# A four-layer graph network on one core: the order of its 11,118 steps, kept as packed data in place of a rule of due times

## The chip, the core and the metric

The kernel runs on one core of a Trainium2 chip. The core has five engines that each work through their own queue of instructions in order: TensorE (PE in the profile) multiplies matrices, VectorE (DVE), ScalarE (ACT) and GpSimd (POOL) do the elementwise work, and SyncE (SP) only issues transfers. 16 DMA engines carry the transfers. TensorE's results go to eight PSUM banks; everything else lives in SBUF, or in DRAM. The metric is the device time of one execution in microseconds (us), the median of several runs.

## What is computed

32 graphs, each with N = 512 nodes, D = 256 features and an adjacency matrix `adj` of 512x512, go through four layers. Every layer ends as `x = layernorm(x + layer(x))`. All numbers are float32.

```
L0  h = relu(((1 + eps) * x + adj @ x) @ W1 + b1);  h @ W2 + b2              # hidden width 512
L1  h = x @ W, 4 heads of 64;  e[i,j] = leaky_relu(e_dst[i] + e_src[j], 0.2)
    softmax over j where adj > 0.5;  attn @ h + bias
L2  q, k, v = x @ Wq.T, x @ Wk.T, x @ Wv.T, 8 heads of 32
    softmax(q.k / sqrt(32) + log(adj + 1e-6)) @ v;  @ Wo.T + bo
L3  s = ((x @ W) @ x.T) * adj;  softmax over the nodes that the mask keeps;  s @ x
```

The kernel adds the logarithm of layer 2 as a factor: `exp(score) * (adj + 1e-6)`. Softmax sums are divided out after the multiplication with v or x.

## The kernel before

**Steps and graphs.** `fast_path` does the work. It does not write instructions at once, but describes them as steps of a `Plan`. A step has a name, an engine, an estimated cost in us, the names of the steps it comes after, the buffers it takes, and a function that emits its instructions. There are 33 sets of steps: one that prepares the weights, and one for each graph, with the same names in each (`s0` to `s7` are the scores of layer 2, `i0` and `i1` the projection of layer 3, `w0` to `w3` its output). In all there are 11,118 steps, 2,077 of them on TensorE. The program keeps several graphs in work at a time: while one graph is in its last layer, others are in the first three, so that TensorE always has a matmul of some graph to do. The stock of buffers limits this: 13 large ones (B), 12 middle ones (C), 10 strips (D), eight PSUM banks (p), 6 graphs alive, 7 score blocks of layer 2 and some more.

**How a graph goes through the engines.** The parts that the prediction speaks of, with their lines:

- The adjacency is loaded twice by SP: as it stands, and turned (`Ar`, L821), in four loads that read 32 columns each in pieces of 128 bytes. A load of x stands at L833.
- Layer 1 builds a row of node values (`R`, L1045 and L1052: written to DRAM, read back to all partitions), ScalarE and VectorE make the weights `z` from it (L1104, L1115), TensorE multiplies.
- Layer 2: eight score steps of four matmuls with 32 rows each into four banks (L1293), ScalarE's exponential (L1306), VectorE's multiplication with the adjacency (L1315), and eight attend steps (L1351). The sums over the keys that the softmax divides by are not all made on TensorE. POOL issues transfers that add one block of 128x2048 numbers (1 MB) to another in SBUF (`collect`, L1326: `cd1`, `cd3`, `cd5`, `cd7`, then `cd2` and `cd6`), and at last one that adds one half of the partitions to the other (`fd0`, `fd1`, L1379). A single TensorE step, `d2` (L1398), takes what is left of both halves, and VectorE applies the result (L1456). Only the very last graph makes these sums wholly on TensorE (L1420).
- The biases of the layers are added to x by POOL's transfers too (`bias_steps`, L625).
- Each layernorm (L655 to L684) makes `rstd` on POOL, `shift` on VectorE, and applies both on ScalarE.
- Layer 3 needs x turned. `turned` writes x to DRAM (L710), reads it back in four loads (L723) into `xL`, and VectorE transposes 32x32 blocks of it (L742) into `xT`. TensorE follows with the projection (`iT`, steps `i0` and `i1`), the scores (`s`, L1539) and the output (`o_ps`); the result is normalised and stored by SP (L1596).

**Modes of TensorE.** A step may run as a whole matmul of 128 columns or as four of 32 columns. Steps marked "any" take the form that is on already; others need one form. `product` does it:

```python
        if plan.mode != "c32":
            nc.tensor.matmul(out, lhsT, rhs, start=start, stop=stop)      # L342
            return
        for q in range(4):
            part = slice(32 * q, 32 * q + 32)
            nc.tensor.matmul(out[part], lhsT[:, part], rhs, start=start, stop=stop)   # L346
```

**What sets the order.** The order of all steps is found while the program is built. `Plan.order` is a list scheduler: it keeps the time at which every engine and buffer comes free by the estimated costs, and takes, among the steps that can start within a short time of the earliest one, the step with the least due time. The due time is the graph's turn times a period of 83.965 us, less the longest chain of steps that still follows, plus shifts by step name. These shifts are written in the call of `plan.run`: one list for all graphs, one for the first graphs, one for the last, and one each for single graphs. `Plan.run` then emits the steps in that order, and every engine does its instructions strictly in that order. A transfer is three steps: its issue on SP or POOL, a step of a made-up engine (`q1` for SP's, `qa` for POOL's accumulates) that stands for its time in the queue, and its landing. The issue and the queue step are ordered each for itself; only the issue is an instruction.

The block after the steps (from L1613) checks whether the fast path's number ranges were kept. If they were not, a second path (`general_path`) would run; it does not run with these inputs.

Of the kernel before, what the change touches and what calls it, by code (L numbers as in the profile page):

```python
# [12 lines left out]
AF = mybir.ActivationFunctionType  # L13
# [3 lines left out]
P = 128  # L17
# [19 lines left out]

class Step:
# [4 lines left out]
    def __init__(self, eng, us, after, take, mode, emit):  # L43
        self.eng, self.us, self.after, self.take, self.emit = eng, us, after, take, emit
        self.mode = mode
        self.then, self.frees = [], []


class Plan:
# [51 lines left out]
    def link(self):  # L101

        self.left = [{} for _ in self.steps]
        for g in reversed(range(len(self.steps))):
            steps, left = self.steps[g], self.left[g]
            for name, s in steps.items():
                for a in s.after:
                    (self.steps[0][a[1:]] if a[0] == "^" else steps[a]).then.append((g, name))
            for k, (_, after) in enumerate(self.frees[g]):
                for a in after:  # L110
                    steps[a].frees.append(k)
        for g in reversed(range(len(self.steps))):
            steps, left = self.steps[g], self.left[g]
            for name in reversed(steps):
                s = steps[name]
                left[name] = s.us + max(
                    (self.left[h][n] + self.hop(s, self.steps[h][n]) for h, n in s.then if h - g < 2),
                    default=0.0,
                )
# [6 lines left out]
    def ready(self, g, name, ends):  # L126

        s, t = self.steps[g][name], 0.0
        for a in s.after:
            h, n = (0, a[1:]) if a[0] == "^" else (g, a)  # L130
            t = max(t, ends[h][n] + self.hop(self.steps[h][n], s))
        return t

    def order(self, period, ahead, window, stay, rush=(), moves=(), edges=(0, (), 0, (), ())):


        room = {b: [(0.0, i) for i in range(n)] for b, n in self.stock.items()}
        engine, mode, out, last = {}, "", [], 0.0
        held = [{} for _ in self.steps]
        ends = [{} for _ in self.steps]  # L140
        waits = [{n: len(s.after) for n, s in steps.items()} for steps in self.steps]
        fwaits = [[len(after) for _, after in frees] for frees in self.frees]
        ready, low, opened = {}, 0, 0
        todo = [len(steps) for steps in self.steps]
        moved = dict.fromkeys((n for steps in self.steps for n in steps), 0.0)
        turn = [max(g - 1, 0) for g in range(len(self.steps))]
        for i, early in enumerate(rush):
            turn[-1 - i] -= early
        for n, far in moves:
            moved[n] += far  # L150
        lead, tail = edges[0], len(self.steps) - edges[2]
        early, late = dict(edges[1]), dict(edges[3])
        own = {g % len(self.steps): dict(far) for g, far in edges[4]}

        def shift(g, name):
            some = early if g <= lead else late if g >= tail else {}
            return moved[name] + some.get(name, 0.0) + own.get(g, {}).get(name, 0.0)

        def near(low):
            fill, until, between, left, drain = ahead  # L160
            return fill if low < until else drain if low >= len(self.steps) - left else between

        def open_to(n):
            nonlocal opened
            while opened < min(n, len(self.steps)):
                for name in self.steps[opened]:
                    if not waits[opened][name]:
                        ready[opened, name] = self.ready(opened, name, ends)
                opened += 1

        open_to(window)
        while low < len(self.steps):
            found = []
            for (g, name), t in ready.items():
                s = self.steps[g][name]
                t = max(t, engine.get(s.eng, 0.0))
                into = self.EITHER.get(mode, "c32") if s.mode == "any" else s.mode
                change = self.CHANGE[into] if s.eng == "pe" and into != mode else 0.0
                for k, (kind, _, rest) in enumerate(s.take):
                    r, n = room[kind], sum(b[0] == kind for b in s.take[:k])  # L180
                    if len(r) <= rest + n:
                        break
                    t = max(t, r[n][0])
                else:
                    due = turn[g] * period - self.left[g][name] + shift(g, name) + stay * change
                    found.append((t, due, g, name, change))
            if not found:
                return math.inf, out
            first = min(found)[0] + near(low)
            _, t, g, name, change = min((due, t, *f) for t, due, *f in found if t <= first)  # L190
            s = self.steps[g][name]
            t += change
            if s.eng == "pe":
                mode = self.EITHER.get(mode, "c32") if s.mode == "any" else s.mode
            del ready[g, name]
            got = {}
            for kind, key, _ in s.take:
                got[key] = held[g][key] = (kind, room[kind].pop(0)[1])
            if s.eng:
                engine[s.eng] = t + s.us  # L200
            end = ends[g][name] = t + s.us
            last = max(last, end)
            out.append((g, name, mode, got))
            for h, n in s.then:
                waits[h][n] -= 1
                if not waits[h][n] and h < opened:
                    ready[h, n] = self.ready(h, n, ends)
            for k in s.frees:
                fwaits[g][k] -= 1
                if not fwaits[g][k]:  # L210
                    key, after = self.frees[g][k]
                    kind, i = held[g].pop(key)
                    free = max(ends[g][a] + self.HOP.get(self.steps[g][a].eng, 0.0) for a in after)
                    room[kind].append((free, i))
                    room[kind].sort()
            todo[g] -= 1
            while low < len(self.steps) and not todo[low]:
                low += 1
                open_to(low + window)
        return last, out  # L220

    def run(self, tries):

        self.link()
        best = min((self.order(*t)[0], t) for t in tries)
        assert best[0] < math.inf
        for g, name, self.mode, got in self.order(*best[1])[1]:
            self.slot[g].update((key, i) for key, (_, i) in got.items())
            self.steps[g][name].emit()
# [3 lines left out]
def fast_path(  # L233
# [24 lines left out]
    B, N, D = x.shape  # L258
    NC = N // P
# [9 lines left out]
    sb = ctx.enter_context(tc.tile_pool(name="sb", bufs=1))  # L269
# [16 lines left out]
    selfw = const.tile([P, P], F32, name="selfw")  # L286
# [21 lines left out]
    def blk(i):  # L308
# [3 lines left out]
    plan = Plan({  # L312
        "B": 13, "C": 12, "D": 10, "p": 8,

        "live": 6, "L0": 1, "L1": 2, "L2": 2, "L3": 1, "AT": 4, "zs": 7, "edge": 1, "tmp": 2,
    })
# [280 lines left out]
    def graph(g):  # L597
        plan.graph()
        slot = plan.slot[-1]
        last = g == B - 1  # L600
        near = g < 2 or g >= B - 3
        t = {"g": g}
# [13 lines left out]
        def little(shape, tag, bufs=2):  # L616
            return small.tile(shape, F32, tag=tag, name=f"{tag}_{g}", bufs=bufs)
# [27 lines left out]
        def norm_steps(n, groups=(range(NC),), into=None):  # L645

            t[f"ve{n}"] = t[f"rstd{n}"] = t[f"shift{n}"] = None
            for k, group in enumerate(groups):
# [8 lines left out]
                @step(f"dev{n}.{k}", "pool", 1.1, (f"va{n}.{k}",) + prev(f"dev{n}.", k))  # L657
                def _(k=k, part=part):
                    if k == 0:
                        t[f"rstd{n}"] = little([P, NC], f"rstd{n}")  # L660
                    nc.gpsimd.tensor_tensor(  # L661
                        t[f"rstd{n}"][:, part], t[f"ve{n}"][:, part], nhalf[:, part], ALU.pow
                    )

                @step(f"sh{n}.{k}", "dve", 0.09, (f"dev{n}.{k}",) + prev(f"sh{n}.", k))
                def _(k=k, part=part):
                    if k == 0:
                        t[f"shift{n}"] = little([P, NC], f"shift{n}")
                    nc.vector.scalar_tensor_tensor(  # L669
                        t[f"shift{n}"][:, part], t[f"mv{n}"][:, part, 0], -1.0, t[f"rstd{n}"][:, part],  # L670
                        op0=ALU.mult, op1=ALU.mult,
                    )
# [1424 lines left out]
```

## Time and profile before

| | |
|---|---|
| median of 3 runs | 2766.87 us (2763.53 to 2771.05) |
| profiled execution | 2767.12 us |
| its span, first to last instruction | 2765.3 us |
| mean granted clock of TensorE | 0.994 |
| DMA traffic | 418.76 MB, mean 151 GB/s |
| read from and written to HBM | 155.53 MB and 31.24 MB |

The profile is of one execution. Its times are in microseconds. Engine names are those above; PEld is TensorE's loading of weights, which lies beside its matmuls. A name such as "iT_ps <- xT" gives the tile that an instruction writes and the ones it reads, by the program's names; L742 is line 742 of the kernel. A list of waits gives, for a group of instructions, the engine and tile that ended the idle time ahead of them, and how long that idle time was. The chain of work that ended last follows the last instruction back to what released it, step by step; its lines give start, length, and what ran. A window's line gives the busy time of each engine within it, the granted clock of TensorE (1.00 is full speed), the share of time that the DMA engines were busy, and GB/s. The hardware queues of SP's transfers are called hardware_dynamic, the queue of POOL's software_dynamic.

### The profile page before, as it was taken

The page shows a single profiled execution, that of the slowest core. Times are in us where ns is not written, and L with a number is a line of the kernel's source. Part 1 is how long each engine was busy: PE and PEld are TensorE (multiplying, and loading weights), DVE is VectorE, ACT ScalarE, POOL GpSimd, SP SyncE. Part 2 cuts the span into 40 slices and gives each one's busy share as a digit, 9 for nine tenths or more (in the row PEclk, how much of TensorE's full clock was granted, in tenths as well). Part 3 has the DMA queues.
Part 4 walks back from the last instruction along what each step waited for, and adds up shares of the span by engine and source line. Part 5 has one row for each costly group of instructions (what it writes and reads, how often), then busy time and mean ns, then how long its engine had stood idle before and what let it go on. Part 6 is the DMA issues. An engine that isn't in the chain of part 4 may idle for free.

```text
span 2765.3 us, 68089 instructions
## 1 busy us (share of the span) xinstructions
PE 2716.7 (98%) x28680; PEld 1317.9 (48%) x28680; DVE 2158.8 (78%) x4257; ACT 1720.4 (62%) x3320; POOL 474.8 (17%) x526
## 2 busy tenths in 40 slices
PE   8999999999999999999999999999999999899998
PEld 6544444444445444445444445444444443444443
DVE  3887778877879877879877879877878877578975
ACT  3676665666666666666666666666665665556853
POOL 1111211121111121111121111121111111111110
PEclk9999999999999999999999999999999999999999
DMA  8487787778888879888878888888896988736760
GB/s 167 80 168 150 148 168 147 160 160 163 158 163 151 171 157 169 162 156 153 174 162 160 149 171 151 171 157 169 155 163 135 182 168 163 156 73 146 155 131 17
DMA packets 476735, 418.76 MB, mean 151 GB/s; under 512 B 377788, under 2 KB 431496, under 8 KB 444552
## 3 DMA queue, kind: packets, MB, share of 16 engines
q0 software_dynamic: 45568, 277.89, 53.1%
q1 hardware_dynamic: 429872, 136.18, 24.2%
q8 instruction: 227, 3.72, 0.5%
q14 instruction: 84, 0.69, 0.1%
q10 hardware_dynamic: 984, 0.28, 0.0%
HBM read 155.53 MB, written 31.24 MB: 68 GB/s over the span
## 4 chain that ended last, share of the span: by engine, by line
PE 86%; DVE 6%; DMA 3%; issue 2%; ACT 1%; POOL 0%; SPq 0%; DVEq 0%; POOLq 0%; ACTq 0%
PE s L1293 8%; PE o_ps L1351 7%; PE v_ps L346 7%; PE y_ps L342 7%; PE o_ps L346 6%; PE o_ps L1137 6%; PE hT_ps L346 6%; PE s L346 5%; PE h1T_ps L346 4%; PE o2p_ps L346 3%; PE iT_ps L342 3%; PE s L342 3%; PE h1T_ps L342 3%; PE kT_ps L342 2%; DVE z L1115 2%; PE qT_ps L346 2%
## 5 line engine op out<-in xcount | busy, mean ns | idle before, releaser
L1315 DVE SCALAR_TENSOR_TENSOR z<-AT,z 128x1024 f32<-128x1024 f32 x512 | 612.6, 1214 | 108.2 <-ACT z L1306 107.0
L1306 ACT ACTIVATE z<-s 128x512 f32<-128x512 f32 x1024 | 541.4, 608 | 109.2 <-PE s L1293 103.4
L1104 ACT ACTIVATE z<-R_bc,nT,S 128x512 f32<-128x512 f32 x512 | 373.4, 807 | 72.0 <-DMA z<-z 58.2
L684 ACT ACTIVATE x<-x,shift,rstd 128x256 f32<-128x256 f32 x508 | 273.9, 593 | 179.6 <-DVE shift L669 174.8
L1115 DVE SCALAR_TENSOR_TENSOR z<-z,T,edge 128x512 f32<-128x512 f32 x512 | 346.5, 742 | 5.8 <-ACT z L1104 5.8
L1326 POOL DMA_DIRECT2D z<-z x186 | 174.4, 942 | 868.4 <-PE o_ps L1351 445.3
L661 POOL TENSOR_TENSOR rstd<-ve,nhalf 128x4 f32<-128x4 f32 (+1 forms) x131 | 169.0, 1339 | 854.8 <-DVE ve L655 846.6
L1293 PE MATMUL s<-qT,kT 32*128 32x512 f32 x2048 | 278.4, 626 | 0.4 <-ACT kT L1264 0.4
L1351 PE MATMUL o_ps<-z,v 128*32 128x512 f32 x2048 | 254.9, 599 | 2.6 <-DVE z L1315 1.4
L1539 DVE TENSOR_TENSOR z<-s,AT 128x512 f32<-128x512 f32 x128 | 88.4, 690 | 214.9 <-PE s L342 110.1
L1137 PE MATMUL o_ps<-z,v 128*32 128x512 f32 x2048 | 233.8, 595 | 2.5 <-DVE z L1115 2.5
L1165 DVE TENSOR_TENSOR z<-z 128x1024 f32<-128x1024 f32 (+1 forms) x256 | 229.5, 949 | 0.7 <-PE o_ps L1137 0.7
L638 DVE BATCH_NORM_STATS2 st<-x 128x6 f32<-128x256 f32 x508 | 212.7, 419 | 10.6
L346 PE MATMUL o_ps<-x,z 128*32 128x257 f32 x3520 | 202.4, 380 | 0.0
L346 PE MATMUL hT_ps<-AT,x 128*32 128x256 f32 (+2 forms) x2640 | 185.5, 380 | 0.0
L342 PE MATMUL y_ps<-w_sb,h1T 128*128 128x256 f32 x832 | 184.4, 379 | 0.0
L342 PEld LDWEIGHTS y_ps<-w_sb,h1T 128*128 128x128 f32 x832 | 156.1, 190 | 21.5 <-issue 1.0
L1293 PEld LDWEIGHTS s<-qT,kT 32*128 32x128 f32 x2048 | 96.7, 184 | 143.5 <-issue 63.6
L346 PEld LDWEIGHTS o_ps<-x,z 128*32 128x32 f32 x3520 | 114.8, 110 | 83.8 <-issue 6.9
L346 PE MATMUL h1T_ps<-hT,w_sb 128*32 128x512 f32 x1296 | 147.9, 595 | 0.0
L625 POOL DMA_DIRECT2D x<-biases x96 | 103.8, 1081 | 237.0 <-issue 67.7
L346 PE MATMUL s<-iT,xT 128*32 128x512 f32 x1232 | 139.4, 592 | 0.1
(188 smaller groups left out, 3858.7 us busy)
## 6 DMA issues: line engine op xcount, KB each, us to landing
z<-z POOLq DMA_DIRECT2D x186, 1024.0 KB, 8.7
x<-biases POOLq DMA_DIRECT2D x96, 512.0 KB, 9.6
R_bc<-R_dram SPq DMA_DIRECT2D x32, 1024.0 KB
Ar<-in_adj_dram SPq DMA_DIRECT2D x124, 256.0 KB
z<-z POOLq DMA_DIRECT2D x62, 512.0 KB, 7.7
x<-in_x_dram SPq DMA_DIRECT2D x32, 512.0 KB
out_dram<-x SPq DMA_DIRECT2D x31, 512.0 KB
x_dram<-x SPq DMA_DIRECT2D x27, 512.0 KB
```

Of the source, the lines that this page charges most:

```text
L342: nc.tensor.matmul(out, lhsT, rhs, start=start, stop=stop)
L346: nc.tensor.matmul(out[part], lhsT[:, part], rhs, start=start, stop=stop)
L638: nc.vector.bn_stats(t[f"st{n}"][:, c, :], t["xo" if n == 4 else "x"][:, c, :D])
L684: nc.scalar.activation(t[into][:, c, :D] if into else xn, xn, AF.Identity, bias=t[f"shift{n}"][:, c : c + 1], scale=t[f"rstd{n}"][:, c : c ...
L1104: nc.scalar.activation(t[f"e{h}"][:, c, :], t["Rbc"][:, h, :], AF.Relu, bias=t["nT"][:, h, c : c + 1], scale=t["S"][:, h, c : c + 1],)
L1115: nc.vector.scalar_tensor_tensor(z, z, t["T"][:, h, c : c + 1], t["edge"][:, c, :], op0=ALU.add, op1=ALU.mult)
L1137: nc.tensor.matmul(po[32 * q : 32 * q + 32, :], t["v"][:, c, hp * P + 32 * q : hp * P + 32 * q + 32], t[f"e{2*hp+q//2}"][:, c, :], start=( ...
L1165: nc.vector.tensor_add(z[:, :m, :], z[:, :m, :], z[:, m : 2 * m, :])
L1293: nc.tensor.matmul(pk, t["k"][hs, o, blk(c)], t["q"][hs, o, :], start=True, stop=True)
L1306: nc.scalar.activation(t[f"E{k}"][:, j, :], t[f"ps{k}{j}"], AF.Exp, scale=QSCALE)
L1315: nc.vector.scalar_tensor_tensor(z, t["AT"][:, c, None, :].to_broadcast([P, 2, N]), ADJ_EPS, z, op0=ALU.add, op1=ALU.mult,)
L1351: nc.tensor.matmul(t[f"n{o}"][32 * j : 32 * j + 32, :], t["v2"][:, c, o * P + F2 * j : o * P + F2 * (j + 1)], t[f"E{k}"][:, j, :], start=( ...
```

## The change

The rule of due times, its tables and the list scheduler are removed. In their place a constant `ORDER` holds the whole sequence of 11,118 steps: base-85 text of compressed bytes. For each place in the sequence it has two bytes, one in the first half of the data and one in the second: how far the step's graph lies ahead of the lowest graph that still has steps left, and the step's place among those that this graph has left. `Plan.sequence` unpacks it, and `Plan.run` follows it. `run` still keeps estimated times, but only to choose which of the free buffers a step gets; and it still sets TensorE's mode from the steps as they come. By its description the sequence was searched in four stretches. A second edit gives the small tiles `rstd` and `shift` of the last layernorm three buffers in place of two.

The steps themselves, their costs and what they come after are unchanged. Read step by step, the sequence has the same 2,077 TensorE steps as before. They stand in another order from the start to TensorE step 1,199, and from step 1,677 to the end; the 478 between them (of graphs 18 to 26, counted from 0) stand as they did. The lines of the kernel after are 31 higher than those before, from `fast_path` on.

```diff
+ORDER = (
+    'c-rk;>6+U}a?Cn$k>J%WX*8=h@%um5W<+Fx==Ip%?;HQJMX9?<0tBkEG9x38VoE6)e*D2FU!IOv>B}q2{ty58$XUlT9(spo`WraM'
...
+)
...
-    def ready(self, g, name, ends):
...
-    def order(self, period, ahead, window, stay, rush=(), moves=(), edges=(0, (), 0, (), ())):
...
+    def sequence(self, text):
+        data = zlib.decompress(base64.b85decode(text))
+        left, low = [list(steps) for steps in self.steps], 0
+        for ahead, place in zip(data[: len(data) // 2], data[len(data) // 2 :]):
+            g = low + ahead
+            yield g, left[g].pop(place)
+            while low < len(left) and not left[low]:
+                low += 1
+        assert low == len(left)
+
+    def run(self, text):
+
+        self.link()
         room = {b: [(0.0, i) for i in range(n)] for b, n in self.stock.items()}
...
+        for g, name in self.sequence(text):
             s = self.steps[g][name]
-            t += change
-            if s.eng == "pe":
-                mode = self.EITHER.get(mode, "c32") if s.mode == "any" else s.mode
...
+            t = engine.get(s.eng, 0.0)
+            for a in s.after:
+                h, n = (0, a[1:]) if a[0] == "^" else (g, a)
+                t = max(t, ends[h][n] + self.hop(self.steps[h][n], s))
             for kind, key, _ in s.take:
-                got[key] = held[g][key] = (kind, room[kind].pop(0)[1])
+                free, i = room[kind].pop(0)
+                t = max(t, free)
+                held[g][key] = kind, i
+                self.slot[g][key] = i
+            into = self.EITHER.get(self.mode, "c32") if s.mode == "any" else s.mode
+            if s.eng == "pe" and into != self.mode:
+                t += self.CHANGE[into]
+                self.mode = into
+            end = ends[g][name] = t + s.us
             if s.eng:
...
+                engine[s.eng] = end
+            s.emit()
...
-        best = min((self.order(*t)[0], t) for t in tries)
-        assert best[0] < math.inf
-        for g, name, self.mode, got in self.order(*best[1])[1]:
-            self.slot[g].update((key, i) for key, (_, i) in got.items())
-            self.steps[g][name].emit()
...
-                        t[f"rstd{n}"] = little([P, NC], f"rstd{n}")
+                        t[f"rstd{n}"] = little([P, NC], f"rstd{n}", 2 + (n == 4))
...
-                        t[f"shift{n}"] = little([P, NC], f"shift{n}")
+                        t[f"shift{n}"] = little([P, NC], f"shift{n}", 2 + (n == 4))
...
-        plan.run([(83.965, (0.0968633, 4, 1000000000.0, 9, 0.0348847), 6, 4.208, ...
+        plan.run(ORDER)
```

## The prediction

> **What bounds the kernel now.** I read the page first, then the chain of work that ended last, then TensorE's waits, then windows, and last SP's and POOL's own instructions.
>
> ```profile
> span 2765.3 us, 68089 instructions
> ...
> PE 2716.7 (98%) x28680; PEld 1317.9 (48%) x28680; DVE 2158.8 (78%) x4257; ACT 1720.4 (62%) x3320; POOL 474.8 (17%) x526
> ```
>
> TensorE is the bound: it is idle for 2765.3 - 2716.7 = 48.6 us in all. The chain shows the beat:
>
> ```profile
> 497.40 7.15 PE v_ps L346 x128
> 580.36 7.15 PE v_ps L346 x128
> 663.33 7.15 PE v_ps L346 x128
> ```
>
> The same piece comes back every 82.97 us, and so up to about 2118 us: one graph per 82.97 us. The window of one beat has no idle TensorE and a full clock, two windows of the last stretch do not (columns: stretch, length, busy time of PE, PEld, DVE, ACT, POOL, PE's clock, DMA share, GB/s):
>
> ```profile
> 497.00:580.00 83.00, 83.00 (x922) 40.14 (x918) 67.77 (x133) 53.40 (x104) 14.23 (x16) 1.00 0.81 156
> 2280.00:2300.00 20.00, 16.55 (x205) 7.37 (x196) 17.75 (x31) 8.82 (x16) 3.56 (x3) 0.91 0.98 154
> 2380.00:2400.00 20.00, 13.04 (x40) 5.12 (x41) 3.76 (x7) 4.02 (x10) 1.68 (x2) 0.83 0.77 153
> ```
>
> So the beat has nothing to give but mode changes, and what a new order can win lies in the filling (to 480 us) and the emptying (from 2124 us). I priced every TensorE step by its start-to-start interval in the beat (score step 0.96, attend step 0.86, FFN, projection or aggregation steps 1.72 to 3.46, output step 1.74, transposes 0.44, a mode change 0.09 to 0.11). The 2077 steps of the old order come to 2685.3 us. What the trace took beyond that:
> - from the first matmul (4.5 us) to 42.3 us: 11.0 (first loads, half clock until 17.7 us). It stays: the same loads come first.
> - 42.3 to 480.3: 15.9.
> - the beat to 2124: 1.8, nearly all at 2121 to 2124, in steps whose order is not changed. It stays.
> - 2124 to the last output step at 2750.7: 34.0, of which the last two waits (0.9) stay, being a chain without other work.
>
> **What the change removes.** The order of both built programs shows that the change does what it says: the same 2077 TensorE steps, in another order up to step 1199 (graph 18, counted from 0) and from step 1677 (graph 26) on; between them nothing moves. Mode changes fall from 541 to 512: 29 at 0.105 us are 3.0 us. No matmul columns, no transfer and no DVE or ACT work is added or taken away; ORDER is read while the program is built. The third buffer for the last layer's rstd and shift adds no instruction. Were every wait of the filling and emptying gone and no other came, the span would be 2765.3 - 3.0 - 15.9 - 33.1 = 2713.3 us. That is the floor. One of the waits is far the longest:
>
> ```profile
> PE iT_ps L346 <- DVE xT L742: 8.0, 1, 8.0
> ```
>
> **What the change adds: transfers come together.** The new order is tight for TensorE, so DMA decides.
>
> ```profile
> q0 software_dynamic: 45568, 277.89, 53.1%
> q1 hardware_dynamic: 429872, 136.18, 24.2%
> ```
>
> POOL's queue moves 277.89 MB in 0.531 x 2765.3 = 1468 us of all 16 engines: 5.5 us for a 1 MB accumulate (collect), 2.8 us for a half one (bias, or fd, the last half of a layer-2 sum). In the trace's landings its 344 transfers all come in the order of issue. The old rule and the new data both let a transfer's queue step stand elsewhere than its issue, so a gap-free plan is no proof. And the beat itself is tight: the last accumulate (L1379) lands 0.4 to 3.7 us before d2, the matmul on it.
>
> (1) The sum before d2. Per graph three accumulates follow each other: cd7, cd6, fd1. In the beat, counted from score step s7: cd7 is issued at 14.1 us; 1.0 issue + 5.5 + 1.8 landing and reissue + 5.5 + 2.8 (a bias ahead) + 2.8 + 2.3 landing give 35.8, the trace has 38.3; so I add 2.5 for SP's traffic. d2 stands at 40.6. The new POOL order gives:
> - graph 0: cd7 cd2 cd6, a bias, fd0, a bias, fd1 = 3 x 5.5 + 4 x 2.8 = 27.7 from 9.0 on: 42.5 against 38.5, 4.0 late.
> - graph 2: cd2 cd7 cd6 and five halves, 30.5 from 12.1 on: 48.4 against 46.4, 2.0 late.
> - graph 28: cd5 and four halves stand ahead of cd7, a bias ahead of fd1: 43.0 against 36.4, 6.6 late.
> Sum 12.6. Bounds: none late (without the 2.5 it is 1.5 + 0 + 4.1 = 5.6) up to twice as much, 25.
>
> (2) The turned x of layer 3: x3 is written to DRAM (L710), read back in four loads (L723), transposed (L742), then iT. One graph of the beat first:
>
> ```profile
> 1363.01 0.57 SPq L710 DMA_DIRECT2D x_dram<-x  x1
> 1370.47 8.34 SPq L723 DMA_DIRECT2D xL<-x_dram  x4
> 1378.99 6.69 SPq L821 DMA_DIRECT2D Ar<-in_adj_dram  x4
> ```
>
> (SP's instructions in order of time: start, length, what.) And from the chain of waits, the place that cost 8 us:
>
> ```profile
> 2363.80 4.56 SPq L723
> 2368.40 5.02 DMA xL<-x_dram
> 2373.42 1.12 DVE edge L1088 x3
> 2374.54 11.47 issue
> ...
> 2386.10 0.72 DVE xT L742
> 2386.82 0.14 issue
> 2386.96 3.41 PE iT_ps L346 x16
> ```
>
> In the beat the four adjacency loads (Ar, 1 MB in 128-byte pieces) stand behind the read; DVE transposes at 1385.2, 7.0 us after the last load is issued at 1378.1. At 2386 four Ar loads and an x load stood right ahead of the write, and the last load, issued at 2368.4, took 17.6. The new SP order puts 3 or 4 Ar loads between write and read for graphs 2, 7, 14, 15, 16 and 26 (the old: never over one). Four cost between 6.7 (SP's own issue time above) and 17.6 - 7.0 = 10.6; I take 8.7, three 6.5. Off come 2.0 that the landing has to spare in the beat (0.0 to 3.4) and the room between the last projection and iT over the beat's 40.5: +9.3, -1.7, +2.6, +1.7, +4.6, -1.0. Late by 0, 8.4, 4.1, 5.0, 0 and 5.5 to 7.5 (a write behind loads too), say 6.5: sum 24. Bounds: 0 (the next graph in the old order, with such loads ahead, did not wait) and 6 x 9.7 = 58 (the shown wait with its slow clock).
>
> (3) The clock. Behind waits of 1.3 to 3.1 us at 212, 2294, 2513 and 2646 us the clock record shows half speed for 3.4 us (the 0.91 windows), 1.7 us of work lost each. Seven waits from (1) and (2): 12; bounds 0 and 9 x 3.4 / 2 = 15. The Trainium skill, "TensorE: Matmul & The Clock Gate", Part 1, has the clock fall after an idle window of about 3.4 us. By that page only the six waits over 3.4 us would pay, an estimate of 10.2 in place of 12; the trace has it behind 1.3 us, so the trace decides.
>
> (4) Small late starts, 0.1 to 1 us, where a bank or an eviction comes a little late: the old order lost about 16 us by these in its 700 unrepeated steps, 0.023 each, and none in the beat. 1550 steps are unrepeated now: between 0 and 35. I take 17, halfway, since the old unrepeated steps and the beat are equally near.
>
> Sum: 2713.3 + 12.6 + 24 + 12 + 17 = 2778.9 us of span. The profiled execution took 2767.12 for a span of 2765.3, so 1.8 lies around it: **2780.7 us**. The median of the runs, 2766.87, is 0.25 below that execution; I leave that out. In the filling and emptying nothing hides these waits: TensorE has no other step in its order, and its queue is strict, so whatever stands behind d2 or iT waits too. DVE has the same: xT behind an unlanded load holds up the scores' multiplications.
>
> The skill's "DMA: Bandwidth & Descriptors", Queues, rings and completion order, says that completion is not FIFO per issuing engine. On POOL's queue this trace never shows it; on SP's only rows of 1 KB overtake. By that sentence a late half could pass others and (1) would shrink to nothing, an estimate of 2768 with the rest as it is.
>
> **Rivals.**
> - *The order holds* (faster). The transfers fit, because room was added elsewhere (graph 2 has 9.3 us more). Then 2713.3 + one wait such as the shown 9.7 + half of (4) 8.5 + 1.8 = 2733. For it: TensorE's order has no hole, and the emptying now has 8 to 10 us more between the last projection and iT than at the place that waited (29.8 there). Against it: the queues above. It decides once the waits of (1) to (4) sum to less than 2758.6 - 1.8 - 2713.3 = 43 us. Chance 0.27.
> - *Gain and loss cancel*: (1) and (2) at half and the clock at five falls: 2713.3 + 6.3 + 12 + 8.5 + 17 + 1.8 = 2758.9, and from there to 2775. Chance 0.13.
> - *Loads run into each other* (much slower): each of the six places costs 10.6 + 1.7, (1) doubles, (4) is 35: 2713.3 + 74 + 25 + 5 + 35 + 1.8 = 2854; half way there is 2817. Against it: a stalled TensorE issues fewer transfers. Chance over 2815: 0.08.
>
> **Numbers.** 0.3% of 2766.87 is 8.3 us, about what a measurement can tell from no change. Forecast, 2775 to 2815: 0.52; above: 0.08; so slower 0.60, same 0.13, faster 0.27. The range leaves out the top 0.08 and the best part of the order holding (under 2733, about 0.12): 2733 to 2815. Its slower part alone is 2775 to 2815.
>
> **What would show it.** TensorE's waits should name the accumulates into z ahead of the two-bank d_ps (L1398) (graphs 0, 2, 28) and DVE xT ahead of iT_ps several times, with a 0.83 or 0.91 clock behind each; between graphs 19 and 25 the beat must still be 82.97 us. If the waits of TensorE sum to under 30 us, and none is over 3 us, I am wrong and the order holds. If waits are many but short, (4) was the size, not the queues.

## The result, and the profile after

| | before | after |
|---|---|---|
| median | 2766.09 us (4 runs, 2763.53 to 2771.05) | 2812.91 us (4 runs, 2810.28 to 2818.31) |
| profiled execution | 2767.12 us | 2818.31 us |
| span | 2765.3 us | 2816.5 us |
| mean granted clock | 0.994 | 0.986 |

The kernel became slower by 46.8 us: the ratio is 1.017, with a 95% interval of 1.0149 to 1.019. The forecast was 2780.7, some 14 us above the kernel before, so the sign was right and the size less than a third of what it is. From the page of the profile after:

```profile
span 2816.5 us, 68977 instructions
...
PE 2726.0 (97%) x29112; PEld 1328.7 (47%) x29112; DVE 2152.0 (76%) x4257; ACT 1714.0 (61%) x3320; POOL 481.0 (17%) x526
```

TensorE is now idle for 2816.5 - 2726.0 = 90.5 us in place of 48.6. Its list of waits says for whom (total, times, longest):

```profile
PE d_ps L1429 <- DMA z<-z: 15.7, 2, 10.1
PE iT_ps L373 <- DVE xT L773: 15.7, 3, 8.2
PE iT_ps L377 <- DVE xT L773: 13.3, 2, 8.3
...
PE y_ps L373 <- DVE y L1241: 4.5, 1, 4.5
PE hT_ps L377 <- DMA x<-in_x_dram: 4.2, 1, 4.2
PE d_ps L1429 <- issue: 3.7, 1, 3.7
```

The first two groups are those that the prediction named: d_ps behind the accumulates into z, three times (graphs 0, 2 and 28), and iT_ps behind xT, five times (graphs 2, 9, 15, 25 and 26; the prediction had not named 9 and 25). The third new thing is a load of x that comes late (graph 17). The beat is untouched, and the stretches behind the waits run at a lower clock (windows: stretch, length, busy time of the engines, clock, DMA share, GB/s):

```profile
1740.00:1823.00 83.00, 83.00 (x922) 40.34 (x918) 67.88 (x134) 53.53 (x105) 14.87 (x16) 1.00 0.88 161
2350.00:2370.00 20.00, 14.77 (x34) 6.93 (x35) 10.94 (x31) 4.34 (x9) 1.93 (x2) 0.74 0.49 89
2580.00:2600.00 20.00, 10.67 (x164) 4.93 (x168) 6.24 (x18) 7.43 (x12) 1.88 (x2) 0.74 0.43 96
```

Two places show how a transfer comes late. First SP around the layer-3 input of graph 7 (start, length, what):

```profile
787.90 0.58 SPq L741 DMA_DIRECT2D x_dram<-x  x1
792.12 16.71 SPq L852 DMA_DIRECT2D Ar<-in_adj_dram  x3
808.99 2.62 SPq L754 DMA_DIRECT2D xL<-x_dram  x3
811.66 0.86 SPq L852 DMA_DIRECT2D Ar<-in_adj_dram  x1
812.56 1.83 SPq L754 DMA_DIRECT2D xL<-x_dram  x1
```

The write had landed by 793.6, but three Ar loads stood ahead of the read, and SP spent 16.71 us on issuing them; the third alone held it for 11.98 us. The prediction had 6.7 to 10.6 us for four. Then POOL around the sums of graph 28 (in brackets: idle time before, and what ended it):

```profile
2544.26 0.86 POOL L1357 DMA_DIRECT2D z<-z  x1 [5.75 <-PE o_ps L1382]
2544.79 1.22 POOL L656 DMA_DIRECT2D x<-biases  x1
...
2546.53 2.15 POOL L656 DMA_DIRECT2D x<-biases  x1
2550.47 0.82 POOL L1410 DMA_DIRECT2D z<-z  x1 [1.79 <-DMA z<-z]
2551.01 1.21 POOL L656 DMA_DIRECT2D x<-biases  x1
2551.58 1.54 POOL L1357 DMA_DIRECT2D z<-z  x1
2571.36 0.86 POOL L1357 DMA_DIRECT2D z<-z  x1 [18.25 <-DMA z<-z]
...
2583.20 0.82 POOL L1410 DMA_DIRECT2D z<-z  x1 [9.90 <-DMA z<-z]
```

These are cd5, four halves (three biases and fd0), cd7, cd6 and fd1. cd6 waits for cd7, which is 19.5 us on its way: cd5 and the four halves, issued just ahead of it, landed one after another from 2555.3 to 2565.9, and cd7 at 2571.1. Then cd6 itself takes 11.6 us, while SP's 1 MB load R_bc, issued at 2571.13, is under way too.

**The ledger** sets each TensorE step's time up to the next step against its price. By the prices of the prediction the new steps come to 2682.2 us, as forecast. Against the floor of 2713.3 the span is 103.2 us longer: 19.4 in waits ahead of d_ps (1); 29.0 + 4.5 + 4.2 = 37.7 in waits for xT, behind xT on VectorE, and for the late x (2); 19.9 of extra time in the steps right behind these waits, at half speed (3); the remaining 26.2 is (4), with some 6 of it inside the three d2 steps. The forecast had 12.6, 24, 12 and 17, which makes 65.6. (The profiled execution is 5.4 us above the median.)

### The profile page after: what moved, and what is told of

The parts are those of the page before. It is cut to its first block, busy times and chain, and to the rows that moved or that the text cites. A ratio compares the mean times of both kernels' runs of the same rounds, so it can differ in the third digit from the quotient of the medians.

```text
span 2816.5 us, 68977 instructions
## 1 busy us (share of the span) xinstructions
PE 2726.0 (97%) x29112; PEld 1328.7 (47%) x29112; DVE 2152.0 (76%) x4257; ACT 1714.0 (61%) x3320; POOL 481.0 (17%) x526
## 3 DMA queue, kind: packets, MB, share of 16 engines
q1 hardware_dynamic: 429872, 136.18, 24.3%
## 4 chain that ended last, share of the span: by engine, by line
PE 47%; DMA 3%; DVE 2%; issue 1%; ACT 1%; SPq 1%; POOL 0%; POOLq 0%; DVEq 0%; ACTq 0%
PE s L1324 5%; PE o_ps L1382 4%; PE o_ps L1168 4%; PE v_ps L377 3%; PE hT_ps L377 3%; PE o_ps L377 3%; PE h1T_ps L377 3%; PE y_ps L373 2%; PE s L377 2%; PE s L373 2%; PE o2p_ps L377 2%; DMA z<-z 2%; PE iT_ps L373 2%; PE y_ps L377 1%; PE kT_ps L373 1%
## 5 line engine op out<-in xcount | busy, mean ns | idle before, releaser
L1337 ACT ACTIVATE z<-s 128x512 f32<-128x512 f32 x1024 | 547.6, 607 | 164.2 <-PE s L1324 158.4
L692 POOL TENSOR_TENSOR rstd<-ve,nhalf 128x4 f32<-128x4 f32 (+1 forms) x131 | 177.8, 1372 | 857.8 <-DVE ve L686 786.0
L1196 DVE TENSOR_TENSOR z<-z 128x512 f32<-128x512 f32 (+1 forms) x256 | 232.3, 951 | 14.3 <-PE o_ps L1168 12.9
L377 PE MATMUL hT_ps<-AT,x 128*32 128x256 f32 (+2 forms) x2736 | 193.1, 383 | 0.0
L377 PEld LDWEIGHTS o_ps<-x,z 128*32 128x32 f32 x3584 | 117.4, 110 | 90.7 <-issue 14.3
L969 ACT ACTIVATE h1T<-h1T_ps,b_sb 128x512 f32<-128x512 f32 x128 | 87.0, 688 | 120.3 <-PE h1T_ps L377 70.6
L373 PE MATMUL y_ps<-w_sb,h1T 128*128 128x256 f32 x656 | 148.4, 385 | 4.5 <-DVE y L1241 4.5
L1168 PEld LDWEIGHTS o_ps<-z,v 128*32 128x32 f32 x2048 | 69.9, 110 | 141.4 <-issue 114.2
L373 PEld LDWEIGHTS y_ps<-w_sb,h1T 128*128 128x128 f32 x656 | 124.8, 193 | 21.7 <-DVE y L1241 5.2
```

The source lines that it names most:

```text
L1168: nc.tensor.matmul(po[32 * q : 32 * q + 32, :], t["v"][:, c, hp * P + 32 * q : hp * P + 32 * q + 32], t[f"e{2*hp+q//2}"][:, c, :], start=( ...
L1196: nc.vector.tensor_add(z[:, :m, :], z[:, :m, :], z[:, m : 2 * m, :])
L1337: nc.scalar.activation(t[f"E{k}"][:, j, :], t[f"ps{k}{j}"], AF.Exp, scale=QSCALE)
```

## The experiments

Ratios are to the kernel before, timed on the same chip. The kernel after (2812.91) was timed apart from the experiments; the median of the kernel before was between 2764.25 and 2766.09 us in every timing. "In the ledger" always means the one profiled execution.

### The four stretches alone

Both orders have done the same steps at four points, so they can be exchanged between them. The expectations name wrong TensorE steps for these points: they lie at steps 335, 751, 1218 and 1675, not at 160, 355, 1199 and 1677. By the same ledger, cut where the points really are, the stretches take 447.9, 540.8, 598.3 and 559.9 us before and 460.3, 553.3, 624.3 and 561.2 after: +12.4, +12.5, +26.1 and +1.3.

```diff
-stretches: new new new (same) new
+s1_only:   new old old (same) old
+s2_only:   old new old (same) old
+s3_only:   old old new (same) old
+s4_only:   old old old (same) new
```

> The kernel after with the new order in its first stretch alone (TensorE steps 0 to 160, about the first 215 us), the old order in all others. Both orders have done the same steps at the borders of the stretches, so they can be exchanged there. Theory A (each stretch brings its own losses, as the ledgers of the two profiles have them: 218.2 us to the border after, 215.1 before): +3 us, 2769. Theory B (the losses come from transfers that one stretch leaves in the queues for the next): under +1 us here, the loss shows only with the new order behind it.

> The new order in the second stretch alone (TensorE steps 160 to 355, about 215 to 480 us). Theory A: 270.8 us in place of 263.4, so +7.4 us, 2773.5, with the waits ahead of d_ps of graph 2 and iT of graph 2 as in the profile after. Theory B: well under that, +3 us or less.

> The new order in the third stretch alone (TensorE steps 355 to 1199, about 480 to 1574 us, where the old order ran its beat). Theory A: 1134.9 us in place of 1095.4, so +39.5 us, 2805, nearly all of the change's loss. Theory B: half of that or less.

> The new order in the last stretch alone (TensorE steps 1677 to 2077, from about 2198 us on). Theory A: 555.9 us in place of 554.7, so +1 us, 2767: what the new order wins by its closer packing (some 29 us of waits that are gone) it loses in three waits of 6 to 10 us (iT of graphs 25 and 26, d_ps of graph 28) with their slow clock. Theory B: the three waits are smaller here, and it is faster than before by 5 us or more.

| stretch | median | against before | ratio (95%) |
|---|---|---|---|
| s1_only | 2780.53 | +16.3 | 1.0058 (1.0041 to 1.0075) |
| s2_only | 2776.81 | +12.6 | 1.0049 (1.0032 to 1.0066) |
| s3_only | 2787.09 | +22.8 | 1.0089 (1.0072 to 1.0106) |
| s4_only | 2759.47 | -4.8 | 0.9987 (0.9977 to 0.9996) |

The four differences add up to 46.9 us, and the whole change costs 46.8. So in the main each stretch carries its own losses: theory A, once the borders are right. It is not exact: s1_only costs 3.9 us more than its ledger, s3_only 3.3 less, and the last stretch by itself is a small gain where the ledger has +1.3, which is nearer to what theory B said of it. There the wait ahead of iT of graph 25 is 2.5 us in the ledger, in place of 8.4 in the kernel after, with the same order but other times at which the transfers meet. Three quarters of the loss, 35.4 us, lie in the second and third stretch (452 to 1591 us), where the old order lost 1.0 us in all by the ledger, so that next to nothing could be won.

### Thin transfers

```diff
-                src, dst = (t[f"E{b}"].rearrange("p h n -> p (h n)") for b in (k, a))
+                src, dst = (t[f"E{b}"].rearrange("p h n -> p (h n)")[:, :N] for b in (k, a))
...
-                    nc.gpsimd.dma_start(z[dst], z[src], accum_op=ALU.add)
+                    nc.gpsimd.dma_start(z[dst, :N], z[src, :N], accum_op=ALU.add)
...
-                        t["Ar"][q].rearrange("j c (b i) -> j c b i", i=32),
...
+                        t["Ar"][q],
+                        adj[g][P * a : P * a + P].rearrange("(c j) n -> j c n", j=32),
```

The first two edits are those of a_pool, a_both and b_pool: they leave out three quarters of the sums of layer 2. The third is that of a_ar and a_both: rows of the adjacency stand where turned ones belong. b_pool has the old order.

> The kernel after with every accumulate of layer 2 (L1357 and L1410: cd and fd) cut to its first quarter: the same instructions and waits, a quarter of the bytes. It leaves out three quarters of the terms that the softmax of layer 2 divides by. Theory 1 (POOL's transfers and SP's share the DMA engines, and the new order lets them meet): the waits ahead of d_ps (28 us of loss with their slow clock) go, and most of the waits ahead of iT, y_ps and hT too (some 58 us), since SP's loads and stores drain faster: 2735 to 2755. Theory 2 (SP's loads hold themselves up, by their order and their small pieces): only the 28 us go, 2785. Theory 3 (engines stand in a wrong order, whatever the transfers cost): within 8 us of 2813.

> The kernel after with the four adjacency loads Ar (L852) in pieces of 2 KB in place of 128 bytes: the same bytes, tiles and instructions, but rows of the adjacency where turned ones belong, so layers work with another adjacency. Theory 1 (the loads' bytes meet POOL's bytes): little, 2800 or more. Theory 2 (the small pieces hold SP's queue up, between the write and the read of x): the waits of graphs 2, 7, 15 and 26 behind Ar loads go, 34 us with their clock, those ahead of d_ps stay: 2779.

> Both edits at once in the kernel after: accumulates of a quarter, Ar loads in pieces of 2 KB. Theories 1 and 2: no wait of TensorE on a transfer is left after 60 us, and the order is near its floor: 2725 to 2740 (2713 is the floor, 1.8 lie around it, and the small late starts, 10 to 20, stay). Theory 3: within 8 us of 2813.

> The old order with the accumulates cut to a quarter (and the third buffer of rstd and shift). If the old order loses to engines and not to transfers, as its list of waits says, little is won: its one wait on a transfer after 60 us (8 us and 1.5 of clock) may go, so 2754 to 2767. If cheap accumulates help whatever the order (theory 3's reading of a gain in the first run), it is faster by as much as the kernel after is.

| kernel | median | against before | ratio (95%) |
|---|---|---|---|
| a_pool | 2727.08 | -38.8 | 0.9860 (0.9840 to 0.9879) |
| a_ar | 2787.38 | +21.5 | 1.0086 (1.0065 to 1.0108) |
| a_both | 2727.82 | -38.0 | 0.9861 (0.9842 to 0.9880) |
| b_pool | 2748.87 | -17.0 | 0.9938 (0.9918 to 0.9957) |

With a quarter of POOL's bytes the new order gains 85.8 us on itself, the old one 17. TensorE's list of waits of a_pool begins with these lines (line numbers shift a little from kernel to kernel with the length of ORDER):

```profile
PE AT_t L880 <- DMA A<-in_adj_dram: 6.8, 3, 3.6
PE hT_ps L369 <- DMA x<-in_x_dram: 5.2, 1, 5.2
PE ok_ps L1645 <- DVE okr L1643: 3.4, 1, 3.4
PE y_t L1231 <- ACT z L1333: 1.1, 2, 0.8
```

The first two lie in the first 17 us, the third at the very end. d_ps and iT are gone as waits on transfers, though not one of SP's loads was changed: on average the write of x3 landed 5.0 us after its issue in place of 8.0, and an Ar load 6.4 in place of 8.2. So theory 1 holds, with a time below its range of 2735 to 2755, and theory 3 falls: with thin accumulates the new order is 21.8 us faster than the old one. Its span, 2725.3, lies 12.0 above the floor.

a_ar falls between theories 1 and 2: 25.5 us faster than the kernel after, of the 34 that theory 2 gave. SP's mean time to issue an Ar load fell from 2.13 to 0.63 us, yet it landed 6.5 us after its issue. From the issue of the write to the landing of the last read, graphs 2, 7, 15 and 26 still took 27.5, 26.7, 27.2 and 29.2 us, the beat takes 20. The small pieces are a part of it; with the accumulates thin they are worth nothing (a_both as a_pool).

### One queue's order alone

```diff
 SP (h_sp), graph 7; graphs 2, 14, 15, 16 and 26 alike
 write of x3 (graph 7)
-Ar loads (graph 11)
 four reads of x3 (graph 7)
+Ar loads (graph 11)
...
 POOL (h_pool), graph 2; graphs 0 and 28 alike
 cd6, fd0
-bias, bias, bias
 fd1
+bias, bias, bias
```

> The kernel after, with SP's order alone changed: for graphs 2, 7, 14, 15, 16 and 26 the adjacency loads Ar that stood between the write of x3 (L741) and its four reads (L754) stand behind the reads. TensorE's, VectorE's, ScalarE's and POOL's orders stay. Step (2) of the prediction (those loads hold up the read): the waits of graphs 2, 7, 15 and 26 go, with their clock 7.9 + 7.5 + 9.8 + 9.0 = 34 us in the ledger, so about 2779. Rival (it is POOL's accumulates that delay write and read, the loads between matter little): under 12 us, 2800 or more.

> The kernel after, with POOL's order alone changed: the biases (x<-biases, half-size accumulates) that stood between cd7 and fd1 of graphs 0, 2 and 28, two, three and one of them, stand behind fd1. Step (1) of the prediction (halves ahead of fd1 delay d2 by about 2.8 us each): the loss at graphs 0 and 2 (7.3 and 8.3 us) nearly goes, that of graph 28 (12.8) falls by 3 to 4: 2813 - 18 = 2795. Rival (the three d2 are late for what stands further ahead in the queue): under 6 us, and biases that come later make new waits.

h_sp took 2786.9 us (1.0084, 1.0064 to 1.0104): 26 us less than the kernel after, of 34. From write to last landing, graphs 2, 7, 15 and 26 now took 20.5, 23.2, 22.3 and 14.3 us (34.5, 30.1, 29.7 and 31.9 in the kernel after), and iT waited 3.4 us in all for xT in place of 29.0:

```profile
PE iT_ps L369 <- DVE xT L769: 3.4, 2, 3.2
```

But a new wait came at d_ps of graph 27, 9.3 us in the ledger, which is about the gap to the 34 (the profiled execution is 8.7 us above the median). At these graphs step (2) is the right mechanism.

h_pool took 2813.64 us (1.0174, 1.0157 to 1.0191), no gain at all, so my 18 us are refuted. Ahead of d_ps the ledger's loss did fall, from 5.6 to 1.7 us at graph 0 and from 7.5 to 1.9 at graph 2; at graph 28 it stayed, 12.3 against 12.0. But right behind graph 2's sum ScalarE now waits (its list of waits from 335 to 360 us):

```profile
ACT z L1131 <- DMA R_bc<-R_dram: 12.1, 1, 12.1
```

The 1 MB load of R_bc of graph 4, issued at 334.3 us, landed 18.9 us later in place of 6.7, and TensorE lost 10.8 us there (349 to 370 us). The biases that had been moved back landed by 340.1, so they held it up only in part. With d2 freed, the work behind it came some 9 us sooner, and with it the next two accumulates, cd1 and cd3 of graph 3, which now fell into the time of the load. POOL in the kernel after, then in h_pool:

```profile
345.33 0.90 POOL L1357 DMA_DIRECT2D z<-z  x1 [19.92 <-ACT z L1337]
349.88 1.01 POOL L1357 DMA_DIRECT2D z<-z  x1 [3.64 <-PE s L1324]
```

```profile
335.61 0.86 POOL L1353 DMA_DIRECT2D z<-z  x1 [10.85 <-ACT z L1333]
340.91 1.00 POOL L1353 DMA_DIRECT2D z<-z  x1 [4.44 <-DVE z L1342]
```

The share of the DMA engines from 330 to 360 us is 0.88 in place of 0.79. A wait that is taken away here moves later transfers onto the next consumer's. How far such things shift shows at iT of graph 25: it waits 3.2 us in place of 8.2, though nothing near it was moved.

### The order of all transfers

r1 keeps the order of TensorE, VectorE and ScalarE of the kernel after, step for step, and gives SP's and POOL's steps (POOL's few computations among them) a new one, found by a search that serves POOL's queue strictly in the order of issue and lets it share the DMA engines with SP's. r2 takes the new order for the first and the last stretch only, with its transfers ordered anew in the same way. The last four are its controls.

```diff
-stretches: new new new (same) new, SP and POOL as in the kernel after
+r1:        new new new (same) new, SP and POOL anew
+r2:        new old old (same) new, SP and POOL anew in the first and last
+s14:       new old old (same) new
+b_tr:      old old old (same) old, SP and POOL anew in the first and last
+s0_only:   old old old (same) old
+r5:        r2 with all engines' steps moved further
```

> The kernel after, with a new order of SP's and POOL's steps throughout, and not one step of TensorE, VectorE or ScalarE moved. The order of transfers was searched for one in which POOL's queue is served strictly in the order of issue and shares the engines with SP's. Theory 1 (all that the change lost is the order of transfers): what a_pool reached with thin transfers comes back with whole ones, 2725 to 2745. Rival (this order of TensorE needs more transfer time at some places than the queues have, whatever their order): still above 2766.

> The new order in the first and the last stretch alone, with SP's and POOL's steps in them ordered anew in the same way; the old order in the second and third stretch, where it ran its beat. Theory 1: 2722 to 2740, faster than both kernels, and at least as fast as the run with all four stretches, since the old second and third stretch have 3 us less of prices and no waits. Rival: no faster than 2759, the last stretch alone.

> The new order as it is in the first and last stretch, the old one in the second and third: r2 without its new transfer order. If stretches add up, as the four single ones did: 2765.5 + 16.3 - 4.8 = 2777, and r2's 2738.8 is then 38 us of transfer order. Rival (r2 is fast because it leaves out the bad stretches): 2745 or less.

> The old order of TensorE, VectorE and ScalarE, with SP's and POOL's steps in the first and last stretch ordered anew, in the same way as for r2. The thin accumulates took 17 us off the old order; so at most that, 2750 to 2760. Rival (the transfers' order alone is worth 27 us, whatever order the engines have): 2740 or less.

> The old order given as data, with the third buffer of the last layer's rstd and shift: no instruction is added, and no wait for those tiles is in the list of waits, so 2763 to 2769, no change. Rival (the buffer itself moves addresses or takes a wait away): over 8 us either way.

> r2 with the steps of all engines moved a little further in the first and last stretch. If the rest of r2's losses are small waits for engines: 4 to 8 us less than r2, 2731 to 2735. If they are transfers that land later than any order allows for: within 4 us of r2's 2738.8.

| kernel | median | ratio (95%) |
|---|---|---|
| r1 | 2765.96 | 0.9995 (0.9983 to 1.0007) |
| r2 | 2738.84 | 0.9903 (0.9886 to 0.9919) |
| s14 | 2773.52 | 1.0031 (1.0020 to 1.0041) |
| b_tr | 2759.51 | 0.9984 (0.9974 to 0.9994) |
| s0_only | 2766.83 | 1.0008 (0.9999 to 1.0018) |
| r5 | 2739.77 | 0.9918 (0.9899 to 0.9937) |

r1 gives back 47 us, all that the change had lost, without moving one step of TensorE, VectorE or ScalarE. It does not reach the 2725 to 2745 of theory 1: iT still waits 13.9 us at graphs 25 and 26, and late loads of x cost 4.2 us of waits behind the start.

```profile
PE iT_ps L370 <- DVE xT L770: 13.9, 2, 8.3
...
PE hT_ps L374 <- DMA x<-in_x_dram: 4.2, 2, 3.3
```

So this order of TensorE needs room for transfers that I did not find; whether another order of transfers has it is not shown.

r2 is faster than both kernels, by 26.6 us against before. Its list of waits begins:

```profile
PE AT_t L836 <- DMA A<-in_adj_dram: 4.3, 3, 3.6
PE hT_ps L325 <- DMA x<-in_x_dram: 3.9, 1, 3.9
PE d_ps L1381 <- DMA z<-z: 3.4, 1, 3.4
```

The first two lie in the first 13 us. s14 shows that r2's gain is not the choice of stretches: the same stretches without the searched order of transfers take 34.7 us more. b_tr shows that it is not the transfers alone either: they are worth 5 us to the old order. Only the two together win. The buffers (s0_only) do nothing that can be told from none. r5, with another order of the engines, ends within 1 us of r2, so this search found nothing more there; whether another order has more is not shown.

## Why the prediction was right in sign and wrong in size

- **What the change is, the prices, the beat, the floor:** right. The steps cost what the prices said, the middle stretch took 601.2 us in both kernels, and where transfers are thin the span comes to 12 us above the floor.
- **The order holds** (rival): its mechanism is real, its condition is not met. The gap-free order of TensorE is worth 21.8 us with thin transfers, and the whole ones take it back and 47 more.
- **(1), the sum before d2:** the three places were right, the term too small: 12.6 forecast (4.0, 2.0 and 6.6 at graphs 0, 2 and 28), 19.4 measured (3.7, 5.6 and 10.1). What failed is "so I add 2.5 for SP's traffic", taken from the beat. Counted from s7 as in the prediction, fd1 landed after 43.3, 52.7 and 47.4 us, where 42.5, 48.4 and 43.0 were worked out. The reading that the halves just ahead of fd1 are to blame is only half true: h_pool freed d2 at graphs 0 and 2, and paid at the next load.
- **(2), the turned x:** the mechanism was right (h_sp), the size not: 24 forecast, 37.7 measured. What failed is the list of places, which named only graphs with Ar loads between write and read. At the six graphs that the prediction named (2, 7, 14, 15, 16 and 26) the waits were 5.1, 4.5, 0, 8.3, 0 and 6.2 us, 24.0 in all and so just as forecast, but by luck: graph 2, forecast at 0, waited 5.1, and graph 14, at 4.1, not at all. "Four cost between 6.7 [...] 10.6; I take 8.7" was too low for most of them. From write to last landing the beat takes about 20 us; graphs 2, 7 and 26 were 14.5, 10.1 and 11.9 above that, graph 15 9.7, graphs 14 and 16 only 3.5. The gap of 13.7 lies at three places that the sum put at nothing: graphs 25 (8.2 us of wait) and 9 (1.2), where the write of x3 itself landed only after 15.0 and 16.2 us (4.8 and 4.0 in a_pool, with thin accumulates), and the load of x of graph 17 (4.2 of wait; 15.5 us to landing, 5.9 in a_pool). The wait of graph 7 showed as y_ps <- DVE y, as "DVE has the same" had it.
- **(3), the clock:** 12 forecast, 19.9 measured; ten falls in place of seven, and the record of half speed is mostly 6.8 us long, twice 10.2, in place of the 3.4 that the term used (the record at the 8 us wait of the old trace, from 2383.2 us, was already 6.8 long).
- **(4), small late starts:** 17 forecast, 26.2 measured, and 12.0 in a_pool. Some 6 of the 26.2 lie inside the three d2 steps and belong to their waits. So the guess was not far off for what the engines do among themselves; the rest goes with the thin accumulates, so it comes from transfers too. One case is x of graph 13, late by 1.1 us: its rstd stands on POOL behind a cd6 that waits for cd7.

So the terms were short by 6.8, 13.7, 7.9 and 9.2 us. What (1) and (2) have in common is that each place was priced with the transfers ahead of it in its own queue and a small allowance from the beat, and nothing stood for both queues being late at once; thin accumulates on POOL's queue alone take away the waits of both terms. The upper bounds of (1), (2) and (4) (25, 58 and 35) held, that of (3), 15, did not. The values were taken nearer to the beat than to the one place of the old trace where it had gone wrong, which cost 8 us of wait.

The Trainium skill, "DMA: Bandwidth & Descriptors", Queues, rings and completion order, says in its paragraph on arbitration that every DMA engine serves the queues it has work for in turn, a packet at a time. That agrees with a_pool, where SP's transfers land earlier (the write 5.0 us after issue in place of 8.0) when only POOL's are cut; what a packet's turn is worth, no run here shows. The sentence of the same section on completion that the prediction weighed did not show on POOL's queue here either (it stands there in the paragraph on the queues of SP and ACT): the 344 transfers of POOL's queue again landed in the order of issue, with 195 overlapping pairs of neighbours.

## What to carry to other kernels

A tight order of the bound engine is worth only what the transfer queues can serve: before believing it, write down for each late consumer what stands ahead of it in its queue and what the other queues move in the same stretch. A price read in a steady beat can be too low for a stretch in which transfers bunch. And exchange such an order stretch by stretch: here one of four was no loss, and three quarters of the damage were done where there was nothing to win.

## What the hardware showed that I had not expected

- An issue can hold its engine as long as a transfer: single Ar loads of 256 KB in pieces of 128 bytes held SP for up to 12.4 us (mean 2.13; 0.63 in pieces of 2 KB), and everything behind them on SP's queue.
- A 512 KB write to DRAM landed between 3.3 and 18.0 us after its issue in one execution, a load of the same size between 3.6 and 24.3.
- A fall of the clock to half speed came behind a wait as short as 1.1 us (at 1100 us), but not behind the one of 1.2 us at 995 us; at the three longest waits, of 8.3 (1518 us), 8.2 (2355) and 10.1 us (2589), the record shows 6.8, 10.2 and 10.2 us of it.
